# A RWKV block on one core: the reciprocal deviation spread over partitions by a DRAM store and repeated reads instead of ScalarE copies

## The chip, the core and the metric

The kernel runs on one core of one Trainium2 chip. Its time is the device time of one execution in microseconds (us). A core has TensorE (PE, matmuls; its weight loads are shown as PEld), VectorE (DVE), ScalarE (ACT), GpSimd (POOL) and SyncE (SP). Each takes its own instructions in program order and waits on semaphores for the others. Transfers are issued here from SP's queue and, a few, from ScalarE's queue, and run on 16 DMA engines.

## The reference, cut to what matters

The input is 8 sequences (batches) of 256 tokens with 512 channels, in float32. Each goes through a time-mixing block and a feed-forward block:

```python
xn = _ln(x, ln1_w, ln1_b); sx = _token_shift(xn, state[:, i1])
xxx = tanh((xn + sx * maa_x) @ maa_w1) @ maa_w2 (per group)
x5 = xn + sx * (maa_stack + xxx)                    # five mixed inputs
w = exp(-exp(time_decay + tanh(x5[1] @ decay_w1) @ decay_w2))
r, k, v, g = x5[3] @ Wr.T, x5[0] @ Wk.T, x5[2] @ Wv.T, silu(x5[4] @ Wg.T)
# 32 heads of 16 channels; s is a 16x16 state per head, step by step over the tokens
out = einsum(r, u * (k outer v) + s);  s = (k outer v) + w * s
att = ((a4 - m) * rsqrt(var + EPS)) * gn_w + gn_b   # normed per head, 16 channels
x = x + att * g @ Wo.T
xn2 = _ln(x, ln2_w, ln2_b); sx2 = _token_shift(xn2, ...)
x = x + sigmoid((xn2 + sx2 * maa_r) @ Wr.T) * (relu((xn2 + sx2 * maa_k) @ Wk.T) ** 2 @ Wv.T)
```

The change concerns the line with `rsqrt(var + EPS)`: for each token and each head there is one number, and all 16 channels of the head are multiplied by it. (The mean is already taken out: the weights of v are centred per head, and so are the start states.)

## The kernel before, in words

Channels lie on the 128 partitions and tokens along the free dimension; 512 channels are 4 blocks of 128, handled in NQ = 2 pairs, `q` = 0 and 1, each a tile of 128 x 2 x 256. A batch b passes three stages, each a Python function that lists its operations: `inputs_of_scan` (norm, mixing, the projections to w, k, v, r, g), `scan` and `rest`. The stages of neighbouring batches overlap.

In `scan` the state runs along the tokens as 16 scans a batch (128 in all). For each, an SP transfer brings `vs` (512 KB: rows of v, first stored to DRAM in `vo` from ScalarE's queue, repeated 16 times), ScalarE writes its first column (L893), VectorE multiplies it by k (L900) and scans (L902), GpSimd multiplies by r (L905), and TensorE gathers four such tiles (L913) into `att`. There are six `vs` tiles, so a `vs` load waits until VectorE's scan has freed its tile.

In `rest` (b = 0 to 6; batch 7, the last, takes another path with a matmul at L954 in it) the steps around the change are, in order: ScalarE squares `att` (L931); TensorE averages the squares over the heads' channels into `pv` (L939); ScalarE takes the root into the first 256 columns of `rs`, which is the tile `sq` of pair 0 (L944); VectorE takes the reciprocal (L946). Now `rs` holds, on partition 32 * blk + r and for each token, the number of one head of block blk. The multiplication needs it on all 128 partitions of a pair's tile, four times 32 rows over. Eight ScalarE copies a pair (L968, 32 partitions x 256 each) do that: into `sq` of pair 1 for q = 0, into a tile of the pool `rk` for q = 1. GpSimd multiplies `att` by it (L970), ScalarE applies gn_w and gn_b (L974, two instructions a pair), GpSimd multiplies by the gate (L979), and TensorE projects with Wo (L400, whose first operand pairs are named `Ws` and `g`). L400 is the helper line of most matmuls, L389 that of all SP transfers. A narrow matmul is issued as four of 32 columns, and a profile record is half of one of them.

The order of the work is written out. The operations are listed as a graph with their engines and costs (`Plan.add`), `TURNS` gives each one its rank, and `Plan.order` places them by rank, engine, dependences, tiles that come free, and the planned landing of transfers, and so fixes each engine's program order. For a transfer the plan takes from `LANDS` two numbers by the name of the tile it writes: the time on a common wire, and what passes from there until the data may be used; the wire starts at the earliest 1.2 us after the issue. The names `rsb_` (the spread tile of q = 1), `sq_` and `rd` stand in that table, though the kernel before has no transfer to them except one late output. At run time nothing goes by the plan's times: an engine starts an instruction when the one before it is through and its semaphores have come. The framework also puts each transfer on one of eight completion semaphores in turn, so that a transfer may have to wait for the one eight before it.

Of the kernel before, what the change touches and what calls it, by code (L numbers as in the profile page):

```python
# [67 lines left out]
class Plan:  # L68
# [5 lines left out]
    LANDS = {"vs__": (2.3, 1.8), "rsb_": (0.9, 2.0), "sq_": (0.9, 2.0), "s": (0.2, 1.9), "vo_": (0.75, 2.2), "vo__": (0.38, 2.2), "o_": (0.75, 1.1), "x": (1.6, 1.7), "xt": (1.6, 1.7), "xs": (0.7, 0.9), "idt": (0.2, 2.2), "rd": (0.4, 1.4)}  # L74
# [40 lines left out]
    def stage(self):  # L115
# [224 lines left out]
def tile_rwkv_block(  # L340
# [30 lines left out]
    def pool(name, n, shape, space=sb):  # L371
        plan.pool(name, [space.tile(shape, F32, tag=f"{name}{i}", name=f"{name}{i}") for i in range(n)])
# [65 lines left out]
    pool("g", 4, [P, 2, T])  # L438
    pool("att", 3, [P, 2 * T + 4])

    pool("vo", 3, [2, P, T], dram)
    pool("vs", 6, [P, 4, T])
    pool("rk", 2, [P, 2, T])
    pool("st8", 6, [P, 4, T])
# [688 lines left out]
```

## Time and profile before

| what | value |
|---|---|
| median of 3 runs (613.27, 613.29, 614.44) | 613.29 us |
| the profiled execution, its own time | 613.54 us |
| its span, first to last instruction | 611.7 us |
| TensorE busy | 599.6 us, 98% |
| VectorE, ScalarE, GpSimd busy | 89%, 84%, 85% |
| TensorE clock granted | 0.997 of full speed |
| moved by DMA | 124.76 MB, 204 GB/s over the span |

Busy time is the time in which at least one instruction of the engine runs. The DMA share of a stretch is the mean busy share of the 16 engines. A row of a group reads: line, engine, operation, tile written <- tiles read, count, durations. "Waits" name the instruction that an idle engine was waiting for.

### The profile page before, as it was taken

The page shows a single profiled execution, that of the slowest core. Times are in us where ns is not written, and L with a number is a line of the kernel's source. Part 1 is how long each engine was busy: PE and PEld are TensorE (multiplying, and loading weights), DVE is VectorE, ACT ScalarE, POOL GpSimd, SP SyncE. Part 2 cuts the span into 40 slices and gives each one's busy share as a digit, 9 for nine tenths or more (in the row PEclk, how much of TensorE's full clock was granted, in tenths as well). Part 3 has the DMA queues.
Part 4 walks back from the last instruction along what each step waited for, and adds up shares of the span by engine and source line. Part 5 has one row for each costly group of instructions (what it writes and reads, how often), then busy time and mean ns, then how long its engine had stood idle before and what let it go on. Part 6 is the DMA issues. An engine that isn't in the chain of part 4 may idle for free.

```text
span 611.7 us, 17692 instructions
## 1 busy us (share of the span) xinstructions
PE 599.6 (98%) x7322; PEld 350.8 (57%) x7322; DVE 545.4 (89%) x489; ACT 514.3 (84%) x1172; POOL 522.3 (85%) x418
## 2 busy tenths in 40 slices
PE   8899999999999999999999999999999999999997
PEld 7576755657544764367553775455654464547464
DVE  6599999999999998899998999999999999996342
ACT  5797689999999999999999798999899789965450
POOL 2889999999899998889998999899999988978030
PEclk9899999999999999999999999999999999999999
DMA  9897777788858777958767687896786677971552
GB/s 289 276 234 170 193 185 209 193 211 195 240 157 232 195 197 234 280 137 243 198 194 213 193 249 188 207 288 165 194 244 168 186 220 208 268 227 33 186 164 91
DMA packets 52495, 124.76 MB, mean 204 GB/s; under 512 B 5824, under 2 KB 11200, under 8 KB 52416
## 3 DMA queue, kind: packets, MB, share of 16 engines
q1 hardware_dynamic: 47904, 119.39, 71.6%
q10 hardware_dynamic: 4512, 4.26, 2.2%
q8 instruction: 57, 0.93, 0.7%
q14 instruction: 22, 0.18, 0.1%
HBM read 115.25 MB, written 8.39 MB: 202 GB/s over the span
## 4 chain that ended last, share of the span: by engine, by line
PE 84%; ACT 5%; DVE 5%; POOL 3%; issue 1%; DMA 0%; ACTq 0%; DVEq 0%; POOLq 0%
PE ps L400 70%; PE ps L913 8%; PE ps L606 2%; PE ps L777 2%; POOL st L905 1%; ACT ps L720 1%; DVE st L902 1%; ACT rk L968 1%; ACT sq L968 1%; POOL g L979 1%; PE ps L855 1%; PE ps L939 0%; DMA xt<-in_x 0%; DVE mix L639 0%; DVE mix L722 0%
## 5 line engine op out<-in xcount | busy, mean ns | idle before, releaser
L902 DVE TENSOR_TENSOR_SCAN st<-wrep,vs 128x1024 f32<-128x1024 f32 x128 | 288.8, 2276 | 4.0 <-ACT wrep L883 2.1
L905 POOL TENSOR_TENSOR st<-st,r 128x1024 f32<-128x1024 f32 x128 | 254.2, 2003 | 11.7 <-DVE st L902 7.1
L900 DVE TENSOR_TENSOR vs<-vs,ps 128x1024 f32<-128x1024 f32 x122 | 143.5, 1207 | 3.0 <-ACT vs L893 3.0
L400 PE MATMUL ps<-Ws,mix 128*32 128x512 f32 (+2 forms) x864 | 115.4, 589 | 0.2 <-DVE o L1026 0.2
L400 PEld LDWEIGHTS ps<-Ws,mix 128*32 128x32 f32 (+1 forms) x864 | 37.6, 116 | 61.8 <-issue 55.7
L737 POOL TENSOR_TENSOR mix<-mix,xn 128x512 f32<-128x512 f32 x62 | 67.0, 1098 | 5.5 <-DVE mix L722 5.3
L400 PE MATMUL ps<-mix,Wv 128*32 128x256 f32 (+1 forms) x808 | 61.6, 381 | 1.8 <-DVE mix L734 1.8
L913 PE MATMUL ps<-st,con 128*32 128x256 f32 x1024 | 62.3, 380 | 0.1
L400 PE MATMUL ps<-mix,Wk 128*32 128x256 f32 (+1 forms) x904 | 60.0, 379 | 0.6 <-DVE mix L722 0.6
L400 PE MATMUL ps<-mix,Wg 128*32 128x256 f32 (+1 forms) x736 | 59.1, 380 | 0.2 <-DVE mix L722 0.2
L400 PE MATMUL ps<-mix,Wr 128*32 128x256 f32 (+1 forms) x712 | 59.0, 380 | 0.0
L400 PE MATMUL ps<-mix,Ws 128*32 128x256 f32 (+1 forms) x688 | 57.7, 379 | 0.5 <-issue 0.5
L400 PE MATMUL ps<-Ws,g 128*32 128x512 f32 (+1 forms) x428 | 56.8, 593 | 0.3 <-POOL g L979 0.2
L627 POOL TENSOR_TENSOR sx<-xn 128x512 f32<-128x512 f32 x31 | 32.3, 1050 | 28.3 <-ACT xn L622 23.6
L652 POOL TENSOR_TENSOR mix<-mix,xn 128x512 f32<-128x512 f32 x44 | 47.6, 1099 | 5.8 <-ACT mix L650 5.6
L400 PEld LDWEIGHTS ps<-mix,Wv 128*32 128x32 f32 (+1 forms) x808 | 39.5, 118 | 20.0 <-DVE mix L734 2.2
L400 PEld LDWEIGHTS ps<-mix,Ws 128*32 128x32 f32 (+1 forms) x688 | 40.5, 123 | 16.0 <-POOL st L905 0.8
L400 PEld LDWEIGHTS ps<-mix,Wk 128*32 128x32 f32 (+1 forms) x904 | 39.0, 113 | 18.1 <-issue 1.5
L400 PEld LDWEIGHTS ps<-mix,Wr 128*32 128x32 f32 (+1 forms) x712 | 39.7, 122 | 16.5 <-issue 1.0
L720 ACT ACTIVATE ps<-ps,vec 128x256 f32<-128x256 f32 x112 | 46.4, 444 | 3.1 <-PE ps L400 1.7
L863 ACT COPY att<-ps 32x256 f32<-32x256 f32 x128 | 46.5, 363 | 2.8 <-PE ps L855 0.7
L913 PEld LDWEIGHTS ps<-st,con 128*32 128x32 f32 x1024 | 32.7, 110 | 27.6 <-issue 5.5
(138 smaller groups left out, 976.5 us busy)
## 6 DMA issues: line engine op xcount, KB each, us to landing
vs<-vo SPq DMA_DIRECT2D x128, 512.0 KB, 5.6
Ws<-in_wo SPq DMA_DIRECT2D x16, 512.0 KB, 5.7
Ws<-in_fr SPq DMA_DIRECT2D x16, 512.0 KB, 5.7
Ws<-in_fk SPq DMA_DIRECT2D x16, 512.0 KB, 6.0
Ws<-in_fv SPq DMA_DIRECT2D x16, 512.0 KB, 5.1
x<-in_x SPq DMA_DIRECT2D x9, 512.0 KB, 6.0
vo<-v ACTq DMA_DIRECT2D x15, 256.0 KB, 5.9
out<-o SPq DMA_DIRECT2D x15, 256.0 KB, 4.7
```

The costliest lines, as they stand in the source:

```text
L400: nc.tensor.matmul(out[i : i + n], lhsT=w[:, i : i + n], rhs=x, start=first, stop=final)
L606: nc.tensor.transpose(ps()[:, m, n * P : (n + 1) * P], xh[n]()[:, k * P : (k + 1) * P], idt())
L627: take(512, [sx], [xn], lambda xn=xn, sx=sx, e=nc.vector if quick else nc.gpsimd: e.tensor_tensor(sx(), xn()[:, :, 0:T], xn()[:, :, 1 : T ...
L652: gp(512, t, [t, xn[q]], lambda q=q, t=t: nc.gpsimd.tensor_tensor(t(), t(), xn[q]()[:, :, 1 : T + 1], ALU.add))
L720: act(256, p_, [p_, vec], lambda g=g, q=q, m=m, p_=p_: nc.scalar.activation(p_()[:, m, :], p_()[:, m, :], AF.Identity, bias=col(f"maa_{g}" ...
L737: gp(512, t, [t, xn[q]], lambda q=q, t=t: nc.gpsimd.tensor_tensor(t(), t(), xn[q]()[:, :, 1 : T + 1], ALU.add))
L777: nc.tensor.matmul(pd()[i : i + 32, 0, :], lhsT=w, rhs=src[k // 2]()[:, k % 2, :], start=(k == begin), stop=(k == end))
L863: act(350, atts[q], [pc], lambda i=32 * (2 * q + m), m=m, q=q, h=32 * h: nc.scalar.copy(atts[q]()[h : h + 32, m, :], pc()[i : i + 32, 0, :]))
L900: dve(4 * T, [vs], [vs, kp], lambda m=m, vs=vs, kp=kp: nc.vector.tensor_tensor(vs(), vs(), kp()[:, m : m + 1, :].to_broadcast([P, 4, T]), ...
L902: dve(4 * T, [st], [w, vs], lambda w=w, vs=vs, st=st: nc.vector.tensor_tensor_scan(st().rearrange("p n t -> p (n t)"), w().rearrange("p n ...
L905: gp(4 * T, st, [st, r], lambda m=m, st=st, r=r: nc.gpsimd.tensor_tensor(st(), st(), r()[:, m : m + 1, :].to_broadcast([P, 4, T]), ALU.mul ...
L913: nc.tensor.matmul(pat()[32 * i : 32 * i + 32, 0, :], lhsT=con()[:, s : s + 32], rhs=done[i]()[:, j, :], start=(j == 0), stop=(j == 3),)
```

## The change

For the batches 0 to 6 the 16 copies of L968 go. Right after the reciprocal a transfer on ScalarE's queue stores `rs` (128 x 256, 131 KB) into a new DRAM tile `rd` of shape 32 x 4 x 256, block by block. Two transfers on SP's queue then read it back, one for each pair: two neighbouring blocks of each of the 32 rows (2 KB in one piece), the 32 rows repeated four times, into the same tiles that the copies wrote (262 KB each). The planned landings of `rsb_`, `sq_` and `rd` are longer, and all of `TURNS` is new: 2552 operations instead of 2643, with 112 copies gone and 21 transfers added.

```diff
-    LANDS = {"vs__": (2.3, 1.8), "rsb_": (0.9, 2.0), "sq_": (0.9, 2.0), "s": (0.2, 1.9), ... "rd": (0.4, 1.4)}
+    LANDS = {"vs__": (2.3, 1.8), "rsb_": (0.9, 4.2), "sq_": (0.9, 4.2), "s": (0.2, 1.9), ... "rd": (0.4, 5.5)}
...
     TURNS = """
-        1 118 15 38 54 77 67 76 58 75 96 64 90 111 2 20 144 166 167 168 31 19 36 35 48 56 33 53 66 32 46 47 34 37 49,
...
     pool("vo", 3, [2, P, T], dram)
+    pool("rd", 2, [32, NK, T], dram)
...
         dve(256, [rs], [rs], lambda: nc.vector.reciprocal(rs()[:, 0:T], rs()[:, 0:T]), 6.25)
+        if not last:
+            rd = new("rd", f"rd{b}")
+            plan.add("ACT", 0.37, [rd], [rs], lambda: nc.scalar.dma_start(
+                out=rd().rearrange("r k t -> k r t"), in_=rs()[:, 0:T]), lag=1.0, kb=131)
...
                 rsb = new("rk", f"rsb{b}_{q}") if q else sqs[1]
-                for n in range(2):
-                    for i in range(4):
-                        rows = slice(32 * i, 32 * i + 32)
-                        act(376, rsb, [rs], lambda blk=2 * q + n, n=n, rows=rows, rsb=rsb: nc.scalar.copy(
-                            by_block(rsb)[rows, n, :], rs()[32 * blk : 32 * blk + 32, 0:T]))
+                dma(rsb, lambda q=q: rd()[:, 2 * q : 2 * q + 2, :].rearrange("r n t -> r (n t)").unsqueeze(0)
+                    .to_broadcast([4, 32, 2 * T]), lambda rsb=rsb: rsb().rearrange("p m t -> p (m t)") if len(rsb().shape) == 3 else rsb(), 262, rd)
                 gp(512, att, [att, rsb], lambda att=att, rsb=rsb: nc.gpsimd.tensor_tensor(
                     att(), att(), by_block(rsb), ALU.mult))
```

The load of `vs`, which is the same in both kernels, reads with this list of dimensions, for comparison:

```python
vo()[m, 32 * i : 32 * i + 32].rearrange("(h j) t -> h (j t)", j=4).unsqueeze(0).to_broadcast([S, HB, 4 * T])   # 16 x 8 x 1024
```

More of the change, by code (lines that the diff above doesn't have):

```diff
@@ L73 @@
     LATENCY = {"PE": 0.24, "DVE": 0.14, "ACT": 0.14, "POOL": 0.1, "DMA": 1.65}
-    LANDS = {"vs__": (2.3, 1.8), "rsb_": (0.9, 2.0), "sq_": (0.9, 2.0), "s": (0.2, 1.9), "vo_": (0.75, 2.2), "vo__": (0.38, 2.2), "o_": (0.75, 1.1), "x": (1.6, 1.7), "xt": (1.6, 1.7), "xs": (0.7, 0.9), "idt": (0.2, 2.2), "rd": (0.4, 1.4)}
+    LANDS = {"vs__": (2.3, 1.8), "rsb_": (0.9, 4.2), "sq_": (0.9, 4.2), "s": (0.2, 1.9), "vo_": (0.75, 2.2), "vo__": (0.38, 2.2), "o_": (0.75, 1.1), "x": (1.6, 1.7), "xt": (1.6, 1.7), "xs": (0.7, 0.9), "idt": (0.2, 2.2), "rd": (0.4, 5.5)}
     SWITCH = {"ACT": 1.3, "PE": 0.12}
```

232 rows, old and new, of the table TURNS are left out of this document.

## The prediction

> **What bounds the kernel now.** I read the page first (busy shares, chain), then the view of the line that goes, then busy time by stretches, then the times that bound the work around the line, then the transfers.
>
> ```profile
> span 611.7 us, 17692 instructions
> ...
> PE 599.6 (98%) x7322; PEld 350.8 (57%) x7322; DVE 545.4 (89%) x489; ACT 514.3 (84%) x1172; POOL 522.3 (85%) x418
> ...
> PE 84%; ACT 5%; DVE 5%; POOL 3%; issue 1%; DMA 0%; ACTq 0%; DVEq 0%; POOLq 0%
> ```
>
> TensorE is busy 98% of the span and is 84% of the chain that ends last, so an edit is worth what it takes from, or adds to, the 12.1 us in which TensorE idles. Busy TensorE could still hide slow matmuls; a gather of 32 records, though, takes the same time wherever the chain lists one late in the run:
>
> ```profile
> 488.95 1.73 PE ps L913 x32
> ```
>
> The line that goes, with those that waited for it:
>
> ```profile
> L968 ACT COPY sq<-sq x56: 387/403/407, 104.8 to 517.1; 32x256 f32<-32x256 f32 x56
> L968 ACT COPY rk<-sq x56: 400/402/412, 106.4 to 515.2; 32x256 f32<-32x256 f32 x56
> ...
>   POOL att L970: 3.2, 3
>   PEld ps L400: 0.7, 2
> ```
>
> 112 copies of 0.402 us are 45.0 us of ScalarE. In the whole run GpSimd waited 3.2 us for them and TensorE's weight loads 0.7 us: nearly all of it is hidden.
>
> How the seven batches stand between the end of the reciprocal (L946) and the first matmul with Wo, which needs the product. The end points come from the timeline, first and last batch of seven; the rows by stretch carry all seven in their labels.
>
> ```profile
> 102.41 1.75 DVE L946 RECIPROCAL sq<-sq 128x256 f32<-128x256 f32 x1
> 120.29 1.06 PE L400 MATMUL ps<-Ws,g 128*32 128x512 f32 x8
> 506.44 1.75 DVE L946 RECIPROCAL sq<-sq 128x256 f32<-128x256 f32 x1
> 528.23 1.07 PE L400 MATMUL ps<-Ws,g 128*32 128x512 f32 x8
> ```
>
> ```profile
> 104.16:120.29 16.13, 15.59 (x269) 11.24 (x260) 15.79 (x12) 15.28 (x36) 16.11 (x12) 1.00 0.64 157
> 167.14:189.76 22.62, 22.62 (x320) 10.29 (x316) 22.47 (x20) 22.07 (x52) 20.02 (x17) 1.00 0.71 191
> 229.16:255.19 26.03, 25.07 (x328) 10.54 (x321) 21.70 (x18) 25.06 (x53) 21.79 (x17) 1.00 0.88 245
> 307.14:328.11 20.97, 20.97 (x304) 9.95 (x300) 18.99 (x17) 20.41 (x47) 17.37 (x13) 1.00 0.78 229
> 389.02:411.54 22.52, 22.52 (x392) 12.49 (x386) 22.20 (x19) 21.21 (x49) 20.89 (x19) 1.00 0.94 245
> 451.04:476.72 25.68, 25.48 (x404) 13.69 (x400) 24.24 (x20) 24.03 (x53) 24.32 (x20) 1.00 0.76 211
> 508.19:528.23 20.04, 20.04 (x312) 9.78 (x301) 19.91 (x13) 19.66 (x39) 19.57 (x14) 1.00 0.81 235
> sum 153.99, PE 152.29 PEld 77.98 DVE 145.30 ACT 147.71 POOL 140.08; mean PE 21.76 PEld 11.14 DVE 20.76 ACT 21.10 POOL 20.01
> ```
>
> The columns are length, PE, PEld, VectorE, ScalarE, GpSimd, clock, DMA share, GB/s. Here ScalarE is busy 96% (147.71 of 153.99), so the copies do stand in a crowded engine; but TensorE idles only 1.70 us in all seven together (153.99 - 152.29). Of the other idle time most lies at the two ends, which the change does not touch:
>
> ```profile
> 0.00:30.60 30.60, 26.73 (x252) 19.94 (x254) 17.75 (x40) 19.49 (x49) 16.89 (x31) 0.94 0.87 283
> 581.10:611.70 30.60, 26.72 (x91) 16.06 (x89) 9.46 (x18) 9.06 (x18) 5.57 (x5) 1.00 0.39 128
> ```
>
> That is 3.87 and 3.88 us. Between them 4.3 us of idle TensorE is left (12.1 - 7.75): the most that any new order could win in the middle.
>
> **The change part by part.** Copies: 45.0 us off ScalarE. From TensorE's side this is worth between 0 and the 1.70 us of its stretches; I take half, -0.9, since VectorE and GpSimd are as full there (145.30 and 140.08) and keep their work.
>
> The store and the reads, by rows:
>
> ```profile
> q1 hardware_dynamic: 47904, 119.39, 71.6%
> ...
> vs<-vo SPq DMA_DIRECT2D x128, 512.0 KB, 5.6
> ...
> vo<-v ACTq DMA_DIRECT2D x2, 128.0 KB, 4.5
> ...
> L389 SPq DMA_DIRECT2D vs<-vo x128: 514/515/637, 25.6 to 532.6; - x128
> L877 ACTq DMA_DIRECT2D vo<-v x15: 366/366/386, 41.7 to 496.1; - x15
> ...
> DMA to landing us min/median/max: 3.1/5.6/11.5
> ...
> L979 POOL TENSOR_TENSOR g<-att,g 128x512 f32<-128x512 f32 x14 | 15.1, 1092 | 1.8 <-ACT att L974 1.7
> L974 ACT ACTIVATE att<-att,vec 128x256 f32<-128x256 f32 x32 | 17.4, 594 | 3.2 <-DVE att L962 2.5 <-POOL att L970 0.6
> ```
>
> After the reciprocal now come: issue on ScalarE 0.37, landing like the 128 KB store of `vo` 4.5, issue on SP 0.52, landing at most like `vs` 5.6, the second read's issue 0.52, GpSimd 1.09, two L974 1.19, GpSimd 1.09: 14.9 us. Both ends of one landing are 3.1 and 11.5.
>
> How a transfer is dealt over the 16 engines no row shows; it is the unknown that matters. Each transfer of the profile on this path (`vo`, `vs`) has 128 or 16 as its outermost count on both sides. The new store is a 4 x 32 x 256 list on the DRAM side, the new read a 4-fold repeat of 32 rows. If they are dealt over 16 engines, they cost what the rows say. If they are dealt along that outermost count, four engines carry them. One engine moves 119.39 MB / (0.716 x 16 x 611.7 us) = 17.0 GB/s. A store is then 1.92 us on each of four engines instead of 0.48, a read 3.85 instead of 0.96: 9.6 us a batch instead of 2.4. The chain grows by 1.44 (store), 2.89 (first read) and 3.35 (the second stands behind it) to 22.6 us. I take four engines, the value nearest to how the lists are written.
>
> [...]
>
> Time there is for the chain: the stretches above, changed by how much TensorE work the new order puts between L939 and the first Wo matmul. Counted at the pace of the gather row (0.054 us a record of 256 columns, twice that for 512), this work goes from 17.0, 27.2, 28.9, 25.0, 27.8, 30.7, 25.0 us for the seven batches to 18.3, 28.9, 25.4, 25.5, 26.6, 35.9, 26.7. So there are 17.4, 24.3, 22.5, 21.5, 21.3, 30.9 and 21.7 us. Against 22.6 batch 0 is short by 5.2 and batches 2, 3, 4, 6 by 0.1 to 1.3. The pair that comes late is needed only by the second half of Wo's sum, 1.73 us of matmuls later: 3.5 us remain in batch 0, nothing elsewhere. Against 14.9 nothing is short anywhere. I take +3.5.
>
> In-order queues. On ScalarE the store waits for the reciprocal; in batch 0 a single 0.44 us instruction stands between root and store, so some 1.7 us of waiting; behind it stand the L893 writes for the next scans. Elsewhere 1.8 to 2.8 us of other work stands there, about a reciprocal's length. 45.0 us freed cover this; without the cover VectorE would wait for L893. On SP the two reads wait for the store to land, and `vs` loads stand behind them; those have 9.4 us or more of VectorE work until they are needed, against 0.52 + 5.6. On GpSimd the L970 that waits for the read holds up the L905 products, and so TensorE's gathers; that is batch 4's danger, where 0.94 of the DMA engines are busy already.
>
> The new turns move every queue. VectorE's and GpSimd's instructions are the same in kind and count, TensorE's work too, with 107 instead of 104 changes between matmul forms: 0 to 0.19 us each, the weight load of the wide form,
>
> ```profile
> L400 PEld LDWEIGHTS ps<-mix,Wr 128*128 128x128 f32 x104 | 19.4, 190 | 3.5 <-issue 0.7 <-DVE att L919 0.4
> ...
> L902 DVE TENSOR_TENSOR_SCAN st<-wrep,vs 128x1024 f32<-128x1024 f32 x128 | 288.8, 2276 | 4.0 <-ACT wrep L883 2.1
> L900 DVE TENSOR_TENSOR vs<-vs,ps 128x1024 f32<-128x1024 f32 x122 | 143.5, 1207 | 3.0 <-ACT vs L893 3.0
> ```
>
> so +0.3. The shortest turn of a `vs` tile (VectorE work between the scan that frees it and the product that needs it, by these rows) falls from 7.2 to 6.0 us, in batch 2, against 6.1 and a ScalarE write of 0.3: +0.4. ScalarE loads one table more; it hides in the freed time.
>
> Sum, against the profiled execution: 613.54 - 0.9 + 3.5 + 0.3 + 0.4 = 616.8 us. That execution lies 0.25 above the median of the runs, so 616.6; I say 616.5.
>
> **The rivals.** (a) Everything is hidden and the new order wins idle time of TensorE, because a ScalarE with 45 us to spare is late nowhere. For it: the 3.2 us in which GpSimd waited for copies. Against it: TensorE's 4.3 us are the ceiling. Two thirds of that: 610.5. It decides if the reads land within 17.4 us in batch 0, which at 14.9 they do.
> (b) The change does nothing measurable: dealt over 16 engines, hidden, and the order neither wins nor loses: 613.1.
> (c) The four engines clog. A batch's 9.6 us on them, added to their share in the seven stretches, goes over the stretch by 3.8, 3.0, 6.5, 5.0, 8.2, 3.4 and 5.8 us (first: 0.64 x 16.13 + 9.6 - 16.13), and every load spread over all engines waits for the slowest. A quarter of the `vs` turns in the new order have 11.5 us or less, that is 5.1 over the 6.4 needed; beyond it go 1.4, 3.1 and 0.7 us. With the forecast's own terms: 616.5 + 5.2 = 621.7. Against it: at a share of 0.94 TensorE was busy for all 22.52 us of the stretch.
>
> **How the numbers follow.** 0.2% of this kernel is 1.2 us, about what a measurement tells from no change. The forecast has 0.42, with a range of its own of 614.6 to 619; (a) 0.26; (b) 0.13; (c) 0.19. Slower: forecast and (c), 0.60 with the part of the forecast's range that falls under the bound taken off; faster 0.27 with the low edge of (b); same 0.13. The range goes from 609, (a) with all 4.3 us, to 624, (c) with half its sum more; beyond are landings of 11.5 one after the other.
>
> **What would show it.** Right: no L968; ScalarE busy near 470 us; read-backs landing in 7 us or more, the second some 3 us behind the first; GpSimd idle before L970 with a transfer as releaser, and TensorE idle before the first Wo matmul of batch 0. Wrong: read-backs in under 6 us and no such idle time, which is (a) or (b); VectorE or L893 waiting for `vs`, which is (c); or idle time in places that have to do with none of these transfers, from the new order alone.

## The result: 639.06 us, and the profile after

The changed kernel takes 639.06 us (median of 4 runs, 637.93 to 642.21) against 613.28 us for the kernel before on the same chip: 1.0439 times as long, 95% interval 1.0417 to 1.0461. The forecast was 616.5 us, with a range from 609 to 624. The side was right and the size was not: +25.8 us in place of +3.2.

The page of the kernel after: span, busy times, the clock by slices, the queues, and the chain that ended last by engine and by line.

```profile
span 636.0 us, 17299 instructions
...
PE 603.6 (95%) x7142; PEld 349.9 (55%) x7142; DVE 546.0 (86%) x489; ACT 473.2 (74%) x1061; POOL 522.7 (82%) x418
...
PEclk9999999999997999999998999999999999999999
...
q1 hardware_dynamic: 49752, 123.06, 71.3%
q10 hardware_dynamic: 5436, 5.18, 2.6%
...
PE 57%; DVE 13%; DMA 13%; ACT 8%; issue 5%; POOL 4%; ACTq 0%; SPq 0%; DVEq 0%; POOLq 0%
```

TensorE's idle time went from 12.1 to 32.4 us (636.0 - 603.6), which is 20.3 of the 24.3 us by which the span grew. The other 4.0 are busy time; the granted clock is lower in two of the 40 slices. In the chain, transfers hold 13% where they held 0%. ScalarE did lose its copies: 473.2 us against 514.3.

The waits of the kernel after: who waited for what, us in total, times, longest.

```profile
ACT att L971 <- POOL att L967: 17.1, 8, 4.0
ACT vs L889 <- DMA vs<-vo: 15.2, 9, 5.0
...
DVE vs L896 <- ACT vs L889: 14.6, 11, 4.2
...
POOL att L967 <- DMA sq<-rd: 9.8, 3, 4.3
...
PE ps L395 <- POOL g L976: 9.3, 3, 4.7
...
PE ps L395 <- DMA Ws<-in_wo: 4.5, 2, 2.5
...
POOL att L967 <- DMA rk<-rd: 4.2, 3, 1.6
```

The lines have moved: L889 is the write into `vs` that was L893, L896 the product that was L900, L967 the product with the spread deviation that was L970, L971 and L976 the former L974 and L979, L395 and L384 the helpers. Three kinds of transfer are late: the two reads (GpSimd's L967), the weights of Wo, and, most of all, the loads of `vs`, which the change did not touch. Before, the write into `vs` waited 1.3 us for loads in the whole run; now it waits 15.2. From the view of the line that issues the loads in the kernel before (who waited for them: us, times; then issue to landing):

```profile
  ACT vs L893: 1.3, 2
...
DMA to landing us min/median/max: 4.2/5.6/11.5
```

Batch 1 shows how that reaches TensorE. These rows are from the timeline, engine by engine (start, length, instruction; in brackets the idle time before it and what ended it):

```profile
174.19 0.55 SPq L384 DMA_DIRECT2D rk<-rd  x1
174.83 0.53 SPq L384 DMA_DIRECT2D sq<-rd  x1
...
179.54 0.54 SPq L384 DMA_DIRECT2D vs<-vo  x1
...
189.79 1.09 POOL L967 TENSOR_TENSOR att<-att,sq 128x512 f32<-128x512 f32 x1 [2.10 <-DMA sq<-rd]
194.42 2.14 POOL L976 TENSOR_TENSOR g<-att,g 128x512 f32<-128x512 f32 x2 [3.54 <-ACT att L971]
...
193.56 0.30 ACT L889 ACTIVATE vs<-s,cm 128x4 f32<-128x4 f32 x1 [4.99 <-DMA vs<-vo]
193.76 1.57 ACT L971 ACTIVATE att<-att,vec 128x256 f32<-128x256 f32 x3
...
196.62 5.35 PE L395 MATMUL ps<-Ws,g 128*32 128x512 f32 x24 [4.69 <-POOL g L976]
```

The second read was issued at 174.83 and came to use at 189.79, some 15 us later. But GpSimd's product was done by 190.9, and L971, which needs it, started only at 193.76: ScalarE stood at L889, next in its queue, for a load of `vs`, the one issued at 179.54. It took 14.0 us from issue to use, where the median landing before was 5.6. So it was in most of the nine waits behind the 15.2 us: with the n-th load counted to the n-th write, the load had been issued 11.6 to 16.2 us before its use in seven of them. The loads are late in landing, not in being issued. So TensorE's stall of 4.69 us ends a chain of a late `vs` load, ScalarE, GpSimd; the read-back, though late too, is not the last in it.

Busy time by stretches around that stall (length, TensorE, weight loads, VectorE, ScalarE, GpSimd, granted clock, DMA share, GB/s):

```profile
193.60:197.60 4.00, 0.98 (x8) 0.33 (x12) 1.87 (x2) 3.76 (x7) 3.18 (x3) 0.77 0.26 103
195.70:202.53 6.83, 5.91 (x28) 1.39 (x32) 4.47 (x2) 6.14 (x16) 6.83 (x5) 0.50 0.49 147
342.53:345.94 3.41, 3.41 (x20) 1.08 (x16) 2.15 (x2) 2.15 (x5) 3.41 (x5) 0.50 1.04 239
```

From 193.60 to 197.60 the DMA share is 0.26, that is 4.2 of 16 engines busy. Of the packets begun then 91 are of 4 KB, as only the `vs` loads have them, at 0.161 us a packet (91 x 0.161 / 4.00 = 3.7 engines), and 20 are of 2 KB at 0.084 us (0.4 engines). For 3.6 of these 4.0 us just four packets were in flight, where the mean had been about 16.4 up to 191.9. Twelve engines have done their parts of the loads under way and stand idle while four work off theirs. The second and third row are the clock: half speed for 6.83 us, from within this stall on, and for 3.41 us after a stall in batch 3.

### The profile page after: what moved, and what is told of

Read it like the earlier page. It is cut to its first block, busy times and chain, and to the rows that moved or that the text cites. A ratio compares the mean times of both kernels' runs of the same rounds, so it can differ in the third digit from the quotient of the medians.

```text
span 636.0 us, 17299 instructions
## 1 busy us (share of the span) xinstructions
PE 603.6 (95%) x7142; PEld 349.9 (55%) x7142; DVE 546.0 (86%) x489; ACT 473.2 (74%) x1061; POOL 522.7 (82%) x418
## 4 chain that ended last, share of the span: by engine, by line
PE 57%; DVE 13%; DMA 13%; ACT 8%; issue 5%; POOL 4%; ACTq 0%; SPq 0%; DVEq 0%; POOLq 0%
PE ps L395 47%; DMA vs<-vo 7%; PE ps L909 6%; DVE st L898 4%; DMA Ws<-in_wo 4%; DVE vs L896 3%; PE ps L602 2%; DMA rk<-rd 2%; DVE sq L942 1%; ACT ps L716 1%; POOL st L901 1%; PE ps L773 1%; POOL mix L733 1%; ACT L940 1%; DVE x L982 1%
## 5 line engine op out<-in xcount | busy, mean ns | idle before, releaser
L896 DVE TENSOR_TENSOR vs<-vs,ps 128x1024 f32<-128x1024 f32 x122 | 143.7, 1207 | 16.4 <-ACT vs L889 14.6
L395 PE MATMUL ps<-Ws,mix 128*32 128x512 f32 (+2 forms) x864 | 115.4, 589 | 0.2 <-DVE o L1023 0.2
L395 PE MATMUL ps<-Ws,g 128*32 128x512 f32 (+1 forms) x416 | 61.9, 643 | 13.8 <-POOL g L976 9.3
L395 PEld LDWEIGHTS ps<-Ws,mix 128*32 128x32 f32 (+1 forms) x864 | 38.5, 116 | 61.4 <-issue 54.7
L395 PE MATMUL ps<-mix,Wv 128*32 128x256 f32 (+1 forms) x808 | 59.7, 380 | 2.8 <-DVE mix L730 1.7
L395 PE MATMUL ps<-mix,Wk 128*32 128x256 f32 (+1 forms) x832 | 58.9, 379 | 0.9 <-POOL mix L733 0.7
L395 PE MATMUL ps<-mix,Wr 128*32 128x256 f32 (+1 forms) x688 | 59.0, 380 | 0.0
L395 PE MATMUL ps<-mix,Ws 128*32 128x256 f32 (+1 forms) x688 | 58.1, 380 | 0.0
L395 PE MATMUL ps<-mix,Wg 128*32 128x256 f32 (+1 forms) x664 | 58.2, 380 | 0.0
L889 ACT ACTIVATE vs<-s,cm 128x4 f32<-128x4 f32 x128 | 36.5, 296 | 21.1 <-DMA vs<-vo 15.2
L395 PEld LDWEIGHTS ps<-mix,Wv 128*32 128x32 f32 (+1 forms) x808 | 38.7, 117 | 20.4 <-DVE mix L730 2.1
L395 PEld LDWEIGHTS ps<-mix,Wr 128*32 128x32 f32 (+1 forms) x688 | 39.3, 123 | 17.5 <-issue 2.5
L395 PEld LDWEIGHTS ps<-mix,Ws 128*32 128x32 f32 (+1 forms) x688 | 39.9, 123 | 16.1 <-ACT mix L646 0.8
L395 PEld LDWEIGHTS ps<-Ws,g 128*32 128x32 f32 (+1 forms) x416 | 19.8, 123 | 52.1 <-issue 33.2
```

The source lines that it names most:

```text
L395: nc.tensor.matmul(out[i : i + n], lhsT=w[:, i : i + n], rhs=x, start=first, stop=final)
L889: act(4, vs, [s0, cm], lambda i=i, blk=blk, vs=vs: nc.scalar.activation(vs()[:, :, 0:1], s0()[:, blk, 4 * i : 4 * i + 4].rearrange("p (n o ...
L896: dve(4 * T, [vs], [vs, kp], lambda m=m, vs=vs, kp=kp: nc.vector.tensor_tensor(vs(), vs(), kp()[:, m : m + 1, :].to_broadcast([P, 4, T]), ...
```

## The experiments

Three causes are to be told apart. The late read-back, the forecast's: the product waits for it. The overloaded engines, the forecast's rival (c): four engines have too much to move, and the other loads come late. The new order: it is worse by itself. Where an expectation below speaks of theories A, B and C, A is that four engines carry the transfers, B the new order, and C a round trip through DRAM that is late however it is dealt. The times of before are from the same chip as the kernel beside them.

**The reads over 16 engines.** `rd` is kept as 4 x 32 x 256; the store is one list of 128 rows, and each read is four transfers of 32 rows.

```diff
-    pool("rd", 2, [32, NK, T], dram)
+    pool("rd", 2, [NK, 32, T], dram)
...
-                dma(rsb, lambda q=q: rd()[:, 2 * q : 2 * q + 2, :]....to_broadcast([4, 32, 2 * T]), ...)
+                for i in range(4):   # inside one step of the plan
+                    nc.sync.dma_start(out=by_block(rsb)[32 * i : 32 * i + 32],
+                                      in_=rd()[2 * q : 2 * q + 2].rearrange("n r t -> r n t"))
```

> The changed kernel with the same bytes dealt over all 16 engines: rd is kept block by block (4 x 32 x 256), so the store is one list of 128 rows, and each read is four transfers of 32 rows instead of one with a fourfold repeat in front. Theory A (four engines carry each store and read; their own lateness and that of the loads beside them is the loss): 612 to 618 us, the waits of GpSimd's L967 for rd under 3 us in all. Theory B (the new order of the work is slower by itself): stays above 630. Theory C (a round trip through DRAM is late however it is dealt): above 625, with the waits for rd near the 14 us of the changed kernel.

Measured: 613.75 us, ratio 1.0023 (1.0009 to 1.0038). The loss is gone but for 0.23%, and no wait of L967 for a read is left, while the computation, the order and the amount read stay. The fault is in how the transfers are dealt.

**No transfers at all.** Store and reads are left out, and L967 multiplies `att` by itself.

> The changed kernel without the store and the reads; L967 multiplies att by itself (the factor 1/deviation is left out), so nothing waits for a transfer. It shows the new order alone, with ScalarE free of the copies. Theory A and C: 609 to 615. Theory B: above 630.

Measured: 613.17 us, ratio 1.0016 (1.0005 to 1.0027). The new order falls as a cause. The run also bounds what the freed ScalarE is worth: with 45 us of copies gone and nothing in their place the kernel is not faster than before.

**The same transfers, not waited for.** Only the operand of L967 changes.

```diff
-                    att(), att(), by_block(rsb), ALU.mult))
+                    att(), att(), att(), ALU.mult))
```

> The changed kernel with the store and the reads as they are, on four engines, but L967 multiplies att by itself (the factor 1/deviation is left out), so no engine waits for the reads. If the loss is the lateness of the reads for L967: 610 to 616. If it is the loads that stand beside and behind them on the four engines (vs for VectorE, Ws for TensorE): 620 to 632, with ScalarE's L889 still waiting some 15 us for vs. If the new order is at fault: above 630.

Measured: 639.07 us, ratio 1.0429 (1.0389 to 1.0469): just what the change costs. Its waits:

```profile
ACT vs L889 <- DMA vs<-vo: 25.4, 11, 8.0
...
DVE vs L896 <- ACT vs L889: 18.4, 12, 6.2
...
PE ps L395 <- DMA Ws<-in_wo: 5.8, 3, 3.5
```

and its TensorE row at the stall of batch 1, from the timeline:

```profile
195.02 8.77 PE L395 MATMUL ps<-Ws,g 128*32 128x512 f32 x64 [4.60 <-POOL g L976]
```

The late read-back falls altogether: with the wait for the reads gone nothing is won, the `vs` loads take over its share (25.4 us in place of 15.2), and the stall of batch 1 stands at 4.60 us in place of 4.69. (What is left of waits for the reads is 2.1 us, by the instructions that next write into their tiles.) The time lies above the 620 to 632 us expected of late loads, in the range that was named for the new order; that the order alone costs nothing is shown by the run before this one.

**An eighth of the bytes.** Both reads fetch 64 of the 512 columns, on four engines, and are waited for.

> The changed kernel with each read cut to an eighth of its columns (64 of 512; the rest of the tile keeps old numbers), still on four engines and still waited for. Theory A (bytes per engine): the reads land in some 5 us and the time falls to 611 to 617. Theory C (fixed latency of store and read): stays above 625.

Measured: 613.45 us, ratio 1.0025 (1.0009 to 1.0040). A fourfold transfer is harmless as such, and so is the round trip through DRAM; it is the amount that four engines carry.

**Copies in the new order.** The eight ScalarE copies of a pair stand in one block at the place of the read.

> The order of the changed kernel without store and reads, but with ScalarE's 16 copies a batch issued at the place where the plan has the reads; everything is computed. It tells whether the 45 us of ScalarE that the change frees are worth anything in this order. If the copies are hidden: as the kernel without transfers, 613 to 614 us. If ScalarE's freed time was the gain that the order lives on: 617 or more, with TensorE waiting for ScalarE.

Measured: 664.13 us, ratio 1.0839 (1.0815 to 1.0863), a miss: a block of 3.2 us on ScalarE holds up what waits behind it (VectorE's L718 waits 19.0 us for ScalarE here). The run tells what a badly placed block costs, and nothing of the worth of the freed time.

**The same reads in the kernel before, into DRAM.** 14 fourfold reads of rows of x go into an unused DRAM tile, issued at the first copy of each pair.

```diff
+                            if read:
+                                nc.sync.dma_start(out=scratch[q][:, 0:E], in_=x[b, 0:32, :].unsqueeze(0).to_broadcast([4, 32, E]))
```

> The kernel before, unchanged in its work and order, with 14 extra transfers that nobody uses: at the first copy of each pair SP moves 32 rows of x, repeated four times in front, into a DRAM scratch of 128 rows of 2 KB. Same bytes and the same four engines as the reads of the change, and no store. If four engines are clogged and so make the loads of vs and Ws late: 622 to 640 us, with L893 waiting for vs. If the loss needs the new order: 613 to 616.

Measured: 612.76 us, ratio 1.0003 (0.9990 to 1.0015). Nothing, against what was expected of overloaded engines. Either the order matters after all, or where the reads write. The next runs separate the two.

**Dealt eightfold and sixteenfold.** As in the kernel that does not wait, the same bytes, with the repeat outermost 8 or 16 times; the store stays as it is.

```diff
-                dma(rsb, lambda q=q: rd()[:, 2 * q : 2 * q + 2, :]....to_broadcast([4, 32, 2 * T]), ...)
+                dma(rsb, lambda: rd()....[0:16].unsqueeze(0).to_broadcast([8, 16, 2 * T]), ...)   # or [0:8], [16, 8, 2 * T]
```

> The changed kernel without the wait (L967 multiplies att by itself, the factor is left out), its store as it is, each read of the same 262 KB dealt eightfold (16 rows repeated 8 times in front) instead of fourfold. If the time goes by bytes per engine, each read is half as long on its engines: 614 to 624 us, against 639 with four engines. If any read-back beside the loads costs the loss: 630 or more.

> The run without the wait (the factor is left out), the store still on four engines, each read one transfer dealt sixteenfold (8 rows repeated 16 times in front, same 262 KB). If the reads are the whole loss: 613 to 614.5 us, as with no transfers. If the store on four engines has a part: 616 or more.

Measured: 616.50 us for eight (ratio 1.0075, 1.0038 to 1.0112) and 613.29 for sixteen (1.0011, 1.0000 to 1.0023), after 639.07 for four. The store, on four engines in the last of these as well, costs nothing.

**Into DRAM, in the new order.** The kernel that does not wait, with the reads written to an unused DRAM tile instead of `sq` and `rk`.

```diff
-                    ... lambda rsb=rsb: rsb().rearrange("p m t -> p (m t)") if len(rsb().shape) == 3 else rsb(), 262, rd)
+                    ... lambda q=q: scratch[q][:, 0:E], 262, rd)
```

> The run without the wait (L967 multiplies att by itself, the factor is left out), with each read sent into a DRAM scratch of 128 rows instead of the SBUF tile: same order, same place in SP's queue, same wait for the store, same fourfold dealing. If the loss comes from four engines being busy with the bytes, whatever the destination: 630 to 640 us. If it comes from writing into SBUF through four engines (which would be why the same traffic to DRAM cost the kernel before nothing): 613 to 617.

Measured: 613.34 us, ratio 1.0009 (0.9998 to 1.0021). The dealing, the source, the bytes and the place in the queue are those of the 639 us kernel; only the destination differs, and the loss is gone.

**Into SBUF, in the order of before.** Two unused fourfold reads of x per batch go into the `sq` tiles, which are dead by then, after the gate product (L979).

```diff
+                    if q:
+                        for t in sqs:
+                            nc.sync.dma_start(out=t(), in_=x[b, 0:32, :].unsqueeze(0).to_broadcast([4, 32, E]))
```

> The kernel before, unchanged in work and order on the four compute engines, with two extra reads a batch that nobody uses: 32 rows of x, repeated four times in front, into the two dead sq tiles, issued by SP at the place of the second gate product (L979). If four-engine writes into SBUF make the loads beside them late in any order: 622 to 640 us and L893 waiting for vs. If only the new order is sensitive to it: 612 to 616.

Measured: 647.70 us, ratio 1.0565 (1.0506 to 1.0625), in the order of before, with all its copies. How its `vs` loads fared, from the view of the helper line that issues them (who waited for them, then issue to landing):

```profile
  ACT vs L893: 23.8, 11
...
DMA to landing us min/median/max: 4.2/7.2/16.5
```

Against the rows of the kernel before (1.3 us of waiting, a median of 5.6) the order and the engines' own instructions are the same. So reads that no instruction uses make the `vs` loads late, in the order of before as in the new one, if four engines write them into SBUF. The loss is above the 622 to 640 us expected; part of it may be that ScalarE's L931, which writes into `sq` next, waits 6.3 us for a read to land.

**The packets by themselves.** Nothing else on ScalarE's queue (q10) has packets of 2 KB, so reads issued from it can be told from all others. In both no instruction uses what the reads bring; they are of x, fourfold, once into SBUF and once into DRAM.

```diff
-                dma(rsb, lambda q=q: rd()[...]....to_broadcast([4, 32, 2 * T]), ...)
+                nc.scalar.dma_start(out=dst, in_=x[b, 0:32, :].unsqueeze(0).to_broadcast([4, 32, E]))   # dst: rsb, or DRAM
```

> The changed kernel without the wait (L967 multiplies att by itself, the factor is left out); the reads take 32 rows of x, repeated four times in front, and are issued from ScalarE's queue instead of SP's. Same bytes, same four engines, another queue. If the vs and Ws loads are late because they stand behind the reads in SP's queue: 613 to 620 us. If they are late because the four engines have too much to move, whoever issues it: 630 or more.

> The kernel with both reads of 32 rows of x, repeated fourfold, issued from ScalarE's queue (631.51 us, where nothing waits for them and the multiplication takes att by itself), with one thing changed: the reads write into DRAM scratch instead of into SBUF. On this queue nothing else has packets of 2 KB, so their duration can be read alone; into SBUF a packet took 0.136 us in the mean (1792 packets) and a pair of reads 11.6 to 18 us. Theory: it is the write into SBUF from four engines that is slow, so the packets take about 0.08 to 0.10 us here, a pair 6 to 8 us, and the time comes back to 613 to 615 us. Rival, the issue from ScalarE's queue itself costs something, or the four engines are as slow into DRAM and the SBUF side only matters to others: packets of 0.13 us or more, and then either 613 to 615 us again (slow packets harm nobody when they go to DRAM) or 620 us or more.

Measured: 631.51 us into SBUF (1.0325, 1.0278 to 1.0372), 613.34 into DRAM (1.0015, 1.0002 to 1.0028). The spans and the row of q10, first of the kernel that writes into SBUF:

```profile
span 631.2 us, 17294 instructions
...
q10 hardware_dynamic: 7284, 8.85, 5.1%
```

and of the one that writes into DRAM:

```profile
span 612.8 us, 17281 instructions
...
q10 hardware_dynamic: 7284, 8.85, 4.3%
```

The same packets and bytes took 5.1% x 16 x 631.2 = 515 us of engine time against 4.3% x 16 x 612.8 = 422. Taken one by one from the trace, the 1792 packets of 2 KB lasted 0.136 us in the mean into SBUF and 0.088 into DRAM, where 95 of 100 took 0.084. Of the 89 us in which such packets were in flight into SBUF, more than four were in flight at once for 5, so both reads of a batch use the same four engines. The 64 packets that each of these has per batch are 8.7 us against 5.6.

**Two engines.** As the SBUF kernel of the last pair, with a twofold repeat: once of 64 rows (partitions 0 to 63 and 64 to 127), once as two transfers of 32 rows (0 to 31 and 32 to 63, then the same from 64). The question is whether the distance between the two copies of a transfer counts, 64 partitions or 32, or whether few engines are slow as such. That two engines carry a twofold transfer is an estimate from the packets of 4 bytes that a fourfold and an eightfold read have, 4 and 8.

```diff
-                nc.scalar.dma_start(out=dst, in_=x[b, 0:32, :].unsqueeze(0).to_broadcast([4, 32, E]))
+                nc.scalar.dma_start(out=dst, in_=x[b, 0:64, :].unsqueeze(0).to_broadcast([2, 64, E]))
...
+                for h in (0, 64):   # the other kernel
+                    nc.scalar.dma_start(out=dst[h : h + 64], in_=x[b, 0:32, :].unsqueeze(0).to_broadcast([2, 32, E]))
```

> The kernel whose reads of x go from ScalarE's queue, waited for by nothing (631.51 us with the fourfold repeat; 0.136 us for a 2 KB packet into SBUF, 0.088 into DRAM; the multiplication takes att by itself), with a twofold repeat of 64 rows: two engines, one walking through partitions 0 to 63, the other through 64 to 127, and 64 packets of 2 KB on each per read instead of 32. [...] Rival, few engines writing into SBUF are slow as such: packets of 0.13 us or more, a pair 17 us or more. The time by itself, 615 to 650 us, is not what tells them apart.

> The same with each read as two transfers with a twofold repeat of 32 rows, one to partitions 0 to 63 and one to 64 to 127: again two engines a transfer, the same bytes, but now the two engines of a transfer walk through partitions 32 apart in step. [...] Rival, few engines are slow as such: the same duration in both, 0.13 us or more. [...] One more transfer a read is issued on ScalarE's queue, some 0.4 us each.

Measured: 669.22 us (1.0933, 1.0877 to 1.0989) and 672.23 us (1.0957, 1.0918 to 1.0996). The packets lasted 0.114 and 0.117 us: next to no difference between 64 and 32 apart, and less than the 0.13 us or more of few engines that are slow as such; both times lie above the 615 to 650 us expected. The distance between the copies is out as the main cause; so is a packet time that only the number of engines fixes (0.136 us with four, 0.114 with two). What the trace does show in the 64-apart kernel: packets beside fewer than two `vs` packets in flight (in the mean over the packet) took 0.098 us, those beside 12 or more 0.137. Into DRAM, in the kernel of the pair above, the same two groups took 0.088 and 0.085. Writes into SBUF are slowed beside the `vs` loads, which write into SBUF too; by what stays open.

The runs together. The third column is the time that one of the loaded engines spends on the two reads of a batch, packets times mean packet time. The fourth is counted from the trace's packets: the time between 95 and 560 us of the span in which only 3 to 5 packets were in flight, in the two-engine kernel 1 or 2.

| kernel | against before | engine time of a batch's reads | few packets in flight |
|---|---|---|---|
| before | - | - | 15.9 us (3 to 5), 38.9 us (1 or 2) |
| four engines, SP's queue, into DRAM | +0.8 us | - | 29.7 us |
| four engines, ScalarE's queue, into DRAM | +0.7 us | 64 x 0.088 = 5.6 us | 30.3 us |
| four engines, ScalarE's queue, into SBUF | +19.1 us | 64 x 0.136 = 8.7 us | 38.1 us |
| the change | +25.8 us | - | 43.8 us |
| two engines, 64 apart, into SBUF | +55.9 us | 128 x 0.114 = 14.6 us | 60.2 us (1 or 2) |

With 5.6 us on each loaded engine nothing is lost; with 8.7 and 14.6 the loss grows. A price per us does not follow. The fourfold reads into SBUF cost 19.1 us from ScalarE's queue, 25.8 in the change, and 35.1 in the order of before (647.70 against 612.57). And in the two-engine kernels the instructions that next write into the tiles wait for the reads themselves. These are the two largest of such waits 64 apart:

```profile
POOL rk L846 <- DMA rk<-in_x: 27.8, 3, 14.2
...
ACT sq L927 <- DMA sq<-in_x: 7.7, 1, 7.7
```

With four engines from ScalarE's queue these waits are 1.8 us in all. So the last row of the table is in part the reads' own lateness and not only that of the other loads.

## Why the prediction was wrong

**Right.** Four engines: the traces show it. The reads added 1848 packets to q1: 14 x 128 of data and 14 x 4 of 4 bytes; the stores 924 to q10, 7 x 128 and 7 x 4; the other transfers have 16 of 4 bytes each (4000 for 250 on q1). The eightfold reads have 8 (1904 packets more on q1 than before, 14 x 128 and 14 x 8), and the four transfers of each read over 16 engines have 16 each (4480 more, 56 x 64 and 56 x 16). In the kernel that issues the fourfold reads from ScalarE's queue no more than four of their packets were in flight at once in 84 of 89 us. ScalarE is busy 473.2 us ("near 470"), GpSimd waits before L967 with a transfer as releaser, and TensorE waits before the first Wo matmul of batch 0, in this row of the timeline after:

```profile
121.66 2.78 PE L395 MATMUL ps<-Ws,g 128*32 128x512 f32 x24 [2.21 <-POOL g L976]
```

In batch 1 the first read was in use at 185.43, without a wait, and the second at 189.79, so the second came at least 4.4 us behind the first; the forecast was some 3.

**The term that fell: +3.5 for the read-back that comes late.** The wait is there, in batch 0 and later: TensorE idles 2.21 us before the first Wo matmul of batch 0, and 0.48 where nothing waits for the reads. But it is worth nothing in the total: without it the kernel takes 639.07 us. The step took the second read to land 3.35 us (3.33 by its own terms, 3.85 - 0.52) behind a first one of 5.6 + 2.89; in batch 1 it took some 15 us from issue to use. What is late next, once it is not waited for, is the `vs` load.

**The step that failed: `vs` loads cost nothing, since "those have 9.4 us or more of VectorE work until they are needed, against 0.52 + 5.6".** 5.6 us was the median landing with no such reads beside it. Beside them the load of batch 1 took 14.0 us from issue to use; with the reads put into the order of before the median was 7.2 and the longest 16.5 us. In place of no cost there are 15.2 us of waiting at L889, and 25.4 when nothing waits for the reads. The forecast priced the engines' time almost rightly: two reads at 17.0 GB/s were 7.7 us on each of four engines, against 8.7 measured. It did not carry this on to every other load, each of which is dealt over all 16 engines (16 packets of 4 bytes each) and is through when the slowest four are (from 193.60 to 197.60, four packets in flight for 3.6 of 4.0 us).

**Rival (c) had that mechanism, at 0.19 and +5.2 us.** The sign that was named for it, the write into `vs` waiting for its load, is what came. Its sum counted only `vs` turns shorter than 11.5 us, from the undisturbed landing again, and left out what stands behind L889 in ScalarE's queue: L971, and with it GpSimd's gate product and Wo. The argument held against it, that TensorE was busy all 22.52 us at a DMA share of 0.94, was wrong in kind. A share is a mean over 16 engines and does not tell how they are loaded: at 0.94 nothing stalled before, and after the change TensorE stands still at 0.26, with four engines full and twelve idle.

**The new order and the copies: -0.9 + 0.3 + 0.4.** Together -0.2, and with no transfers the kernel came out at +1.0 us (0.3 to 1.7). Small, and a loss: the 45 us of freed ScalarE time won nothing that can be measured. Rival (a) falls with it, also where the reads do no harm (613.75 us).

**Left out: the clock.** About 10.2 us at half speed (6.83 + 3.41), so up to 5 us, in part within the 4.0 us of added busy time. (The profiled execution of before had a stretch of its own in its first 30.60 us, clock 0.94 there.) No term stood for that.

**Open:** why packets into SBUF are slower beside other loads, and what of the 25.8 us belongs to the reads' own length and what to its echoes (the late `vs`, the late Wo weights, the clock), which the runs only show together. No version here beats the kernel before; the best that computes everything, with the reads over 16 engines, is 0.23% slower.

## What to carry to other kernels

Count the outermost dimension of every transfer before pricing it: here it told how many engines carry it (4 packets of 4 bytes for a count of 4, 8 for 8). Where such a transfer wrote into SBUF, the price was paid by the loads that are dealt over all engines (639.06 us when the reads were waited for, 639.07 when not); into DRAM it was under 1 us (0.8 and 0.7). Hold the time on the loaded engines, not the mean DMA share, against the slack of the other loads, and follow the first late load through the in-order queue of the engine that waits for it. When an engine off the critical path is relieved, as ScalarE was by 45 us here, do not count on the relief itself: here it was worth nothing.

## What was not expected of the hardware

A transfer on four engines is nearly free into DRAM (613.34 us) and costs 26 us into SBUF (639.07), with the same source, bytes and place. And the clock: in the stall of 4.69 us in batch 1 the granted clock fell to 0.50 for 6.83 us, when TensorE had been idle for 3.8 us (195.70 - 191.93). In batch 3 it fell to 0.50 for 3.41 us, 1.2 us after the end of a stall of only 2.49 us (342.53 - 341.31), while with one of 2.89 us it stayed at 1.00. TensorE's rows of the timeline:

```profile
341.31 4.91 PE L395 MATMUL ps<-Ws,g 128*32 128x512 f32 x28 [2.49 <-DMA Ws<-in_wo]
...
491.13 1.07 PE L909 MATMUL ps<-st,con 128*32 128x256 f32 x16 [2.89 <-ACT v L804]
```

The two stretches at half speed start 146.8 us apart. The length of a stall alone did not decide here, 2.49 us against 2.89; what did was not shown.
